# Expert weights by rank: W2 loaded in order of first use, W1 by id for 40 batches, b2's rows spread by GpSimd

## The chip, the cores and the metric

One core of one Trainium2 chip. The metric is device time in microseconds (us) of the kernel, median of its runs. The engines: TensorE (PE; PEld is its weight load), VectorE (DVE), ScalarE (ACT), GpSimd (POOL), SyncE (SP, which here only issues DMAs).

## What is computed

`x` is 128 batches of 128 x 512 float32; each batch has a language id, and each of `L = 10` languages its own small layer.

```python
w1 = W1[language_ids]                       # 512 x 128
w2 = W2[language_ids]                       # 128 x 512
h = relu(einsum('bsh,bha->bsa', x, w1) + b1[language_ids][:, None, :])
adapted = einsum('bsa,bah->bsh', h, w2) + b2[language_ids][:, None, :]
y = x + adapted
mean, var over the last axis of y
normed = (y - mean) * rsqrt(var + 1e-5)
out = x + normed * gamma[language_ids][:, None, :] + beta[language_ids][:, None, :]
```

## The kernel before, in words

A batch is one tile of 128 rows (partitions) by 512. Its steps, and the engine that does each:

- TensorE transposes x in four pieces (`transpose_x`, L235), ScalarE copies the result out of PSUM (`copy_xT`, L239).
- `down` (L258): four float32 matmuls with W1 of the batch's language. ScalarE applies relu and b1 (`relu`, L266).
- `up` (L275): the matmul with W2, read from `w2` at an offset that comes from the language id in a register.
- b2 is added in one of three ways: GpSimd adds it to x ahead of time (`add_b2`, L245, r = x + b2), or VectorE adds it to the result (`vector_b2`, L285), or TensorE adds it as a matmul that picks the row (`up`, L274). `b2_by_vector` and `b2_by_matmul` say which.
- VectorE: `residual` (L292, adds r or x and sums), `scale` (L358, minus the mean, times gamma), `finish` (L367, times the deviation, plus o). ScalarE: the squares (L315) and the root. GpSimd: `add_beta` (L252, o = x + beta).
- SyncE stores o in pairs of batches (L371) and loads x four batches at a time (`load_x`, L71).

gamma, beta (times -0.5 for gamma) and b2 have to stand on all 128 partitions (`gamma_b`, `beta_b`, `b2_b`, each 10 x 512 wide). At the start their 30 rows are split in three bfloat16 parts, and for each row a matmul with a picking column (`spread`, L206) spreads it over the partitions; VectorE (L211) or ScalarE (L209) copies it out of PSUM. The order is written out by hand ahead of the loop, beta's rows first, then gamma's, then b2's.

The loop `for i in range(3, B + U)` runs one batch per turn, software-pipelined: x of batch i, `down` of i-1, `up` of i-2, residual of b = i-3, `finish` one or two batches later; `add_b2(b + 2)` and `add_beta(b)` stand at the start of a turn. `keep` chains the instructions of each engine in program order, so that the scheduler changes nothing in it, the DMAs on SyncE's queue included. Buffers that set how far engines can run apart: 4 groups of x, 4 tiles r, 5 pairs o, 5 PSUM tiles of the result.

W1 reaches `down` in two ways. For batches 0 to 8 SyncE loads the matrix of the batch's own language from memory (`load_first`, L154, the id in a register). From batch 9 on ScalarE copies it (`stage_w1`, L226, 128x512) out of all ten, which lie in SBUF: `w1e` up to batch 20 (rows in the order "(p k)"), `w1` after. All of W2 is loaded at the start in two DMAs (L158).

A last stage (`tail`) finishes batches 124 to 127, partly on GpSimd (`by_pool`, L415, L417).

Of the kernel before, what the change touches and what calls it, by code (L numbers as in the profile page):

```python
# [16 lines left out]
P = 128  # L17
G = 4
EPS = 1e-5
FIRST = 9  # L20
EARLY = 21
LATE = 12
U = 2
# [3 lines left out]
def cond_resid_kernel(ctx: ExitStack, tc: tile.TileContext, x, itok, W1, b1, W2, b2, gamma, beta, out):  # L27
# [49 lines left out]

    ids = const.tile([1, B], I32, name="ids")
# [3 lines left out]
    w1e = const.tile([P, L, KC, A], FP, name="w1e")  # L82
    w2 = const.tile([P, L * H], FP, name="w2")
    x_0 = xp.tile([P, G, H], FP, tag="x", name="x_0")
    xs[0] = x_0

# [3 lines left out]

    keep(nc.sync.dma_start(out=ids, in_=itok.rearrange("(o b) -> o b", o=1)))
    keep(nc.scalar.dma_start(out=rows[0:L, :], in_=beta))
    keep(nc.sync.dma_start(out=rows[L : 2 * L, :], in_=gamma))
    keep(nc.scalar.dma_start(out=rows[2 * L : 3 * L, :], in_=b2))
    load_part(0, 2)
    keep(nc.scalar.dma_start(out=b1r, in_=b1))

    warm = const.tile([P, 1], FP, name="warm")
    keep(nc.vector.memset(warm, 1.0))
    keep(nc.scalar.activation(warm, warm, AF.Abs_reciprocal_sqrt))  # L100
    def load_w1(k):
        keep(
            nc.sync.dma_start(out=w1[:, :, k, :], in_=W1[:, k * P : (k + 1) * P, :].rearrange("l p a -> p l a"))
        )

    ident = const.tile([P, P], FP, name="ident")
    make_identity(nc, ident)
    eps = const.tile([P, 1], FP, name="eps")
    nc.gpsimd.memset(eps, EPS)
    ones = const.tile([P, P], BF, name="ones")  # L110
    nc.gpsimd.memset(ones, 1.0)

# [13 lines left out]

    wrap = const.tile([1, B], I32, name="wrap")
    keep(nc.vector.tensor_scalar(wrap, ids, 0, L, ALU.is_lt, ALU.mult))
    lang = const.tile([1, B], I32, name="lang")
    keep(nc.vector.tensor_tensor(lang, ids, wrap, ALU.add))  # L130
    keep(nc.vector.tensor_scalar(lang, lang, 0, L - 1, ALU.max, ALU.min))

    def lid(b, engine):
        g = b // G
        if (g, engine) not in lids:
            loads, vals = nc.values_load_multi_w_load_instructions(  # L136
                lang[0:1, g * G : (g + 1) * G],
                engines=[engine],
                min_val=0,
                max_val=L - 1,  # L140
                skip_runtime_bounds_check_because="clamped on the chip to 0..L-1 above",
            )
            for ins in loads:
                keep(ins)
            lids[g, engine] = vals
        return lids[g, engine][b % G]

    def load_first(b):
# [4 lines left out]
    def load_w2(lo, hi):  # L156
        dst = w2[:, lo * H : hi * H].rearrange("p (l h) -> p l h", l=hi - lo)
        keep(nc.sync.dma_start(out=dst, in_=W2[lo:hi].rearrange("l a h -> a l h")))  # L158

    def load_early(lo, hi):  # L160
        dst = w1e[:, lo:hi].rearrange("p l k a -> p l (k a)")
        keep(nc.sync.dma_start(out=dst, in_=W1[lo:hi].rearrange("l (p k) a -> p l (k a)", k=KC)))
# [8 lines left out]
    xs[1] = xp.tile([P, G, H], FP, tag="x", name="x_1")  # L171
    for b in (G, G + 2):
        load_part(b, b + 2)
        load_first(b)
        load_first(b + 1)
    xs[2] = xp.tile([P, G, H], FP, tag="x", name="x_2")
    load_part(2 * G, 2 * G + 2)
    load_early(0, 5)
    load_first(2 * G)
    load_early(5, L)  # L180
    load_part(2 * G + 2, 3 * G)

    left = rp.tile([P, H], FP, tag="r", name="left")
    keep(nc.vector.tensor_copy(parts[0:R, :], rows[0:R, :]))
    keep(nc.vector.tensor_tensor(left[32 : 32 + R, :], rows[0:R, :], parts[0:R, :], ALU.subtract))
    keep(nc.vector.tensor_copy(parts[32 : 32 + R, :], left[32 : 32 + R, :]))
    keep(nc.vector.tensor_tensor(left[64 : 64 + R, :], left[32 : 32 + R, :], parts[32 : 32 + R, :], ALU.subtract))
    keep(nc.vector.tensor_copy(parts[64 : 64 + R, :], left[64 : 64 + R, :]))

# [6 lines left out]


    beta_b = const.tile([P, L * H], FP, name="beta_b")
    gamma_b = const.tile([P, L * H], FP, name="gamma_b")
    b2_b = const.tile([P, L * H], FP, name="b2_b")  # L200

    def spread(r, copier):
        t = (beta_b, gamma_b, b2_b)[r // L]
        row = p_y.tile([P, H], FP, tag="y", name=f"row_{r}")
        pick_r = pick[:, r : r + 1].to_broadcast([96, P])
        keep(nc.tensor.matmul(row, lhsT=pick_r, rhs=parts[:96, :], start=True, stop=True))  # L206
        dst = t[:, r % L * H : (r % L + 1) * H]
        if copier is nc.scalar:
            keep(nc.scalar.copy(dst, row))  # L209
        else:  # L210
            keep(nc.vector.tensor_copy(dst, row))  # L211

    xT, hT, rs, os, ys, ssqs, nmeans, rstds = {}, {}, {}, {}, {}, {}, {}, {}
    phs, pxs, sums = {}, {}, {}


    def b2_by_matmul(b):
        return b in (5, B - 1)

    def b2_by_vector(b):  # L220
        return b < 4 or 8 <= b < B - 8 and (b % 4 == 1 if b < 24 else b % 16 in (1, 6, 11) or b % 32 == 30)

    def stage_w1(b):
        w1s[b] = wp.tile([P, KC, A], FP, tag="w1s", name=f"w1s_{b}")
        src = (w1e if b < EARLY else w1).rearrange("p l k a -> p (l k a)")[:, bass.ds(lid(b, ET.Activation) * (KC * A), KC * A)]
        keep(nc.scalar.copy(w1s[b].rearrange("p k a -> p (k a)"), src))  # L226

    def transpose_x(b):
        pxs[b] = p_x.tile([P, KC, P], FP, tag="xT", name=f"pxT_{b}")
        for k in range(KC):  # L230
            if b < EARLY:
# [36 lines left out]
    def up(b):  # L268
        v = lid(b, ET.PE)
        ys[b] = p_y.tile([P, H], FP, tag="y", name=f"py_{b}")  # L270
        m = b2_by_matmul(b)
        if m:
            pick_b = pick[:, bass.ds(v + 2 * L, 1)].to_broadcast([96, P])
            keep(nc.tensor.matmul(ys[b], lhsT=pick_b, rhs=parts[:96, :], start=True, stop=False))  # L274
# [214 lines left out]

    spin(9, H)  # L490
    spin(1, H // 2)

    def spread_turn(lo, hi):
        for r in range(lo, hi):
            spread(r, nc.scalar if r % 7 in (1, 3, 5) else nc.vector)

    def x_turn(b):
        transpose_x(b)
        copy_xT(b)

    x_turn(0)
    transpose_b1()
    spread_turn(0, 4)
    x_turn(1)
    spread_turn(4, 11)
    down(0)
    relu(0)
    spread_turn(11, 15)
    down(1)
    relu(1)  # L510
    x_turn(2)
    spread_turn(15, 19)
    x_turn(3)
    down(2)
    relu(2)
    spread_turn(19, 24)
    down(3)
    relu(3)
    spread_turn(24, R)
    up(0)  # L520
    up(1)

    for i in range(3, B + U):
        b = i - U - 1
        if b > G and b % G == 2 and b // G + 3 < NG:
            load_x(b // G + 3)
        if i == 5:
            load_x(3)
        if i in (8, 10, 12, 14):
            load_w1((i - 8) // 2)  # L530
        if i == 4:
            up(2)
        if i == 5:
            up(3)
        if i > 3 and on(i):
            transpose_x(i)
        if b <= E:
            add_b2(b + 2)
            add_beta(b)
        if i > 4 and on(i - 1):  # L540
            down(i - 1)
        if i > 3 and on(i):
            copy_xT(i)
        if b == 2:
            scalar_means(0)
            deviation(0)
        if i > 4 and on(i - 1):
            relu(i - 1)
        if i + 1 >= LATE and on(i + 1):
            stage_w1(i + 1)  # L550
        if i > 5 and on(i - U):
            up(i - U)
# [37 lines left out]
        if 0 < g and b <= E and half == 1:  # L590
            scalar_means(g)
            deviation(g)
        if FIRST <= i + 1 < LATE:
            stage_w1(i + 1)

        for n, engine in ((i + 3, ET.Activation), (i - U + 3, ET.PE), (b + 1, ET.DVE), (b + 5, ET.Pool)):
            if on(n):
                lid(n, engine)


# [35 lines left out]
```

## Time and profile before

| | |
|---|---|
| median of 3 runs | 308.49 us (308.26 to 308.88) |
| profiled execution, span from first to last instruction | 306.5 us |
| busy, share of the span: PE, DVE, ACT, POOL | 96, 97, 92, 93% |
| granted TensorE clock, mean | 0.989 |
| `add_beta` L252, 128 times; `add_b2` L245, 97 times | 173.9 and 135.7 us in records that overlap |
| `stage_w1` L226 ScalarE copy, mean of one | 612 ns |
| DMA moved | 77.85 MB, mean 254 GB/s |

The profile is of one execution, and its span is the only time that it gives of it: what lies ahead of the first and behind the last instruction makes the rest of the 308.49 us of the runs. A line of a group gives the source line, the engine, what is written from what, and the times. A line of a wait reads "who waits <- who ended it: us in total, times, longest". In the table of stages "(x12)" is a count of instructions. Names carry no buffer numbers: `r`, `o`, `x` stand for all of their kind, `b_b` for `b2_b`.

### The profile page before, as it was taken

The page shows a single profiled execution, that of the slowest core. Times are in us where ns is not written, and L with a number is a line of the kernel's source. Part 1 is how long each engine was busy: PE and PEld are TensorE (multiplying, and loading weights), DVE is VectorE, ACT ScalarE, POOL GpSimd, SP SyncE. Part 2 cuts the span into 40 slices and gives each one's busy share as a digit, 9 for nine tenths or more (in the row PEclk, how much of TensorE's full clock was granted, in tenths as well). Part 3 has the DMA queues.
Part 4 walks back from the last instruction along what each step waited for, and adds up shares of the span by engine and source line. Part 5 has one row for each costly group of instructions (what it writes and reads, how often), then busy time and mean ns, then how long its engine had stood idle before and what let it go on. Part 6 is the DMA issues. An engine that isn't in the chain of part 4 may idle for free. (4 is left out here: it accounts for less than half of the span.)

```text
span 306.5 us, 6981 instructions
## 1 busy us (share of the span) xinstructions
PE 294.6 (96%) x1835; PEld 220.0 (72%) x1835; DVE 295.9 (97%) x771; ACT 282.3 (92%) x777; POOL 283.9 (93%) x238
## 2 busy tenths in 40 slices
PE   8999999999999999999999999999999999999960
PEld 3748787777777777777777777777777777777730
DVE  6889999999999999999999999999999999999985
ACT  3858999999999999999999999999999999999981
POOL 1349899999999999999999999999999999999994
PEclk9999999999999999999999999999999999999995
DMA  6999999976678766766777666767776666773324
GB/s 231 379 390 388 373 371 354 387 231 240 221 255 276 250 202 241 226 257 219 259 276 243 213 209 238 265 224 260 275 238 206 226 231 242 246 266 137 135 109 171
DMA packets 43769, 77.85 MB, mean 254 GB/s; under 512 B 1961, under 2 KB 7348, under 8 KB 43730
## 3 DMA queue, kind: packets, MB, share of 16 engines
q1 hardware_dynamic: 43382, 76.84, 72.1%
q10 hardware_dynamic: 348, 0.57, 0.5%
q8 instruction: 15, 0.25, 0.3%
q14 instruction: 24, 0.20, 0.2%
HBM read 43.85 MB, written 33.55 MB: 253 GB/s over the span
## 5 line engine op out<-in xcount | busy, mean ns | idle before, releaser
L252 POOL TENSOR_TENSOR o<-x,beta_b 128x512 f32<-128x512 f32 x128 | 173.9, 1395 | 10.2 <-DVE beta_b L211 9.5
L245 POOL TENSOR_TENSOR r<-x,b_b 128x512 f32<-128x512 f32 x97 | 135.7, 1399 | 7.3 <-DVE b_b L211 6.2
L258 PE MATMUL ph<-xT,w1s 128*128 128x128 f32 x1024 | 135.4, 275 | 0.0
L275 PE MATMUL py<-w,hT 128*128 x256 | 131.2, 595 | 0.5 <-DVE b_b L211 0.5
L258 PEld LDWEIGHTS ph<-xT,w1s 128*128 128x128 f32 x1024 | 124.9, 192 | 1.0 <-ACT hT L266 0.5
L235 PEld LDWEIGHTS pxT<-ident,x 128*128 128x128 f32 x512 | 66.6, 151 | 65.3 <-issue 49.2
L358 DVE SCALAR_TENSOR_TENSOR py<-py,nmean,gamma_b 128x512 f32<-128x512 f32 x126 | 95.0, 754 | 0.9 <-ACT sq L399 0.8
L367 DVE SCALAR_TENSOR_TENSOR o<-py,rstd,o 128x512 f32<-128x512 f32 x122 | 91.2, 748 | 0.0
L315 ACT ACTIVATE sq<-py,sum 128x512 f32<-128x512 f32 x124 | 85.9, 693 | 2.8 <-DVE py L292 2.5
L235 PE MATMUL pxT<-ident,x 128*128 128x128 f32 x512 | 78.2, 276 | 0.0
L239 ACT COPY xT<-pxT 128x512 f32<-128x512 f32 x128 | 74.7, 584 | 3.5 <-PE pxT L235 3.5
L292 DVE SCALAR_TENSOR_TENSOR py<-py,r 128x512 f32<-128x512 f32 x97 | 67.0, 691 | 0.2
L226 ACT COPY w1s<-w 128x512 f32 x107 | 65.5, 612 | 0.0
L266 ACT ACTIVATE hT<-ph,b1T 128x128 f32<-128x128 f32 x128 | 46.9, 366 | 7.9 <-PE ph L258 2.6
L275 PEld LDWEIGHTS py<-w,hT 128*128 128x128 f32 x256 | 39.1, 192 | 2.9 <-issue 1.0
L315 ACT ACTIVATION_READ_ACCUMULATOR sq<-py,sum 128x1 f32 x124 | 25.0, 202 | 0.0
L292 DVE SCALAR_TENSOR_TENSOR py<-py,x 128x512 f32<-128x512 f32 x31 | 21.7, 699 | 0.4
L285 DVE TENSOR_TENSOR py<-py,b_b 128x512 f32<-128x512 f32 x29 | 20.2, 695 | 0.7 <-PE py L275 0.6
L325 ACT ACTIVATE root<-ssq,eps 128x2 f32<-128x2 f32 x62 | 16.4, 265 | 0.0
L292 DVE DVE_READ_ACCUMULATOR py<-py,r 128x1 f32 x97 | 13.7, 141 | 0.0
L306 ACT ACTIVATE nmean<-sum 128x2 f32<-128x2 f32 x62 | 12.3, 198 | 0.0
L329 DVE SCALAR_TENSOR_TENSOR part<-ssq,root 128x2 f32<-128x2 f32 x62 | 9.3, 151 | 0.2 <-ACT root L325 0.2
(55 smaller groups left out, 90.4 us busy)
## 6 DMA issues: line engine op xcount, KB each, us to landing
out_dram<-o SPq DMA_DIRECT2D x61, 512.0 KB, 3.4
x<-in_x_dram SPq DMA_DIRECT2D x29, 1024.0 KB, 6.2
x<-in_x_dram SPq DMA_DIRECT2D x6, 512.0 KB, 8.8
w1e<-in_L_cond_W_dram SPq DMA_DIRECT2D x2, 1280.0 KB, 12.3
w<-in_L_cond_W_dram SPq DMA_DIRECT2D x4, 640.0 KB, 8.1
w1s<-in_L_cond_W_dram SPq DMA_DIRECT2D x9, 256.0 KB, 8.4
w<-in_L_cond_W_dram SPq DMA_DIRECT2D x1, 1792.0 KB, 10.3
w<-in_L_cond_W_dram SPq DMA_DIRECT2D x1, 768.0 KB, 5.4
```

Of the source, the lines that this page charges most:

```text
L226: keep(nc.scalar.copy(w1s[b].rearrange("p k a -> p (k a)"), src))
L235: keep(nc.tensor.transpose(pxs[b][:, k, :], cols, ident))
L239: keep(nc.scalar.copy(xT[b], pxs.pop(b)))
L245: keep(nc.gpsimd.tensor_tensor(rs[b], xb(b), b2_b[:, bass.ds(v * H, H)], ALU.add))
L252: keep(nc.gpsimd.tensor_tensor(os[g][:, j, :], xb(b), beta_b[:, bass.ds(v * H, H)], ALU.add))
L258: nc.tensor.matmul(phs[b], lhsT=w1s[b][:, k, :], rhs=xT[b][:, k, :], start=(k == 0), stop=(k == KC - 1))
L266: keep(nc.scalar.activation(hT[b], phs.pop(b), AF.Relu, bias=b1T[:, bass.ds(lid(b, ET.Activation), 1)]))
L275: keep(nc.tensor.matmul(ys[b], lhsT=hT[b], rhs=w2[:, bass.ds(v * H, H)], start=not m, stop=True))
L292: nc.vector.scalar_tensor_tensor(ys[b], ys[b], 1.0, r, ALU.mult, ALU.add, accum_out=col(sums, b))
L315: nc.scalar.activation(sq, ys[b], AF.Square, bias=col(sums, b), scale=-float(H), accum_out=col(ssqs, b))
L358: nc.vector.scalar_tensor_tensor(ys[b], ys[b], col(nmeans, b), gamma_b[:, bass.ds(v * H, H)], ALU.add, ALU.mult)
L367: nc.vector.scalar_tensor_tensor(o, ys.pop(b), rstds[g][:, j : j + 1], o, ALU.mult, ALU.add)
```

## The change

- W2: instead of two large DMAs, ten DMAs of one language each, in the order in which the languages first appear. The order is worked out on the chip: for each language the first batch that has it (`seen`, `first`, VectorE), its rank among them (a matmul, `above` with `accum_out`), and from the ranks a row `slots` that holds for each place the language, and for each batch its place. SyncE reads the first, TensorE the second, in `up`. The ids are therefore on ten partitions, one for each language, and GpSimd makes the constants with `iota`.
- W1: loaded by id for batches 0 to 39 into a ring of 7 tiles; `w1e` is gone, `stage_w1` starts at batch 40, and `w1` is loaded in turns 16, 21, 26 and 31 rather than 8, 10, 12 and 14.
- b2: one DMA brings all ten rows to partition 0 of `b2_b`, and two `partition_broadcast` on GpSimd, each of 2560 words, spread them. They stand ahead of GpSimd's first add. The spread by matmul stays for 20 rows (beta, gamma), alternately copied by VectorE and ScalarE; the last 9 of them stand in the turns 3 to 5 of the loop.
- b2 of batches 0 to 3 by matmul rather than by VectorE; that of batch 5 by GpSimd rather than by matmul.
- The three casts for the bfloat16 parts become two copies on ScalarE and a subtraction that writes bfloat16. 6 idle matmuls at the start rather than 10.

```diff
-FIRST = 9
-EARLY = 21
-LATE = 12
+BY_ID = 40
+RING = 7
...
-    wp = ctx.enter_context(tc.tile_pool(name="wp", bufs=5))
+    wp = ctx.enter_context(tc.tile_pool(name="wp", bufs=RING))
...
+    keep(nc.scalar.dma_start(out=b2_b[0:1, :], in_=b2.rearrange("(o l) h -> o (l h)", o=1)))
...
+    nc.gpsimd.iota(weight, [[-16, B + 1]], base=16 * B, channel_multiplier=-1)
+    nc.gpsimd.iota(lang[:, B : B + 1], [[0, 1]], base=0, channel_multiplier=1)
+    nc.gpsimd.iota(count[:, 0:L], [[1, L]], base=0, channel_multiplier=0, allow_small_or_imprecise_dtypes=True)
+    nc.gpsimd.iota(count[:, L : L + 1], [[0, 1]], base=0, channel_multiplier=1, allow_small_or_imprecise_dtypes=True)
...
+    keep(nc.vector.scalar_tensor_tensor(seen, lang, own, weight, ALU.is_equal, ALU.mult))
+    keep(nc.vector.tensor_reduce(first, seen, mybir.AxisListType.X, ALU.max))
+    def rank_languages():
+        order = p_s.tile([P, H], FP, tag="s", name="order")
+        keep(nc.tensor.matmul(order[:L, 0:L], lhsT=first.to_broadcast([L, L]), rhs=ident[:L, :L], start=True, stop=True))
+        keep(nc.vector.tensor_tensor(rows[32 : 32 + R, :], rows[0:R, :], upper(rows, 0), ALU.subtract))
+        keep(nc.vector.tensor_scalar(above, order[:L, 0:L], first, None, ALU.is_gt, ALU.add, accum_out=rank))
+        keep(nc.vector.tensor_scalar(own_of, lang[:, 0:B], own, None, ALU.is_equal))
+        keep(nc.vector.tensor_scalar(place, count[:, 0:L], rank, None, ALU.is_equal))
+        keep(nc.vector.tensor_tensor(parts[64 : 64 + R, :], rows[32 : 32 + R, :], upper(rows, 32), ALU.subtract))
+        keep(nc.scalar.copy(parts[0:R, :], upper(rows, 0)))
+        keep(nc.scalar.copy(parts[32 : 32 + R, :], upper(rows, 32)))
+        return order
+    def place_languages(order):
+        keep(nc.tensor.matmul(order[:1, L : 2 * L], lhsT=own, rhs=place, start=True, stop=True))
+        keep(nc.tensor.matmul(order[:1, 2 * L : 2 * L + B], lhsT=rank, rhs=own_of, start=True, stop=True))
+        keep(nc.vector.tensor_copy(slots, order[:1, L : 2 * L + B]))
...
-    load_w2(0, 3)
-    load_first(0)
-    load_first(1)
-    load_part(2, G)
-    load_first(2)
-    load_first(3)
-    load_w2(3, L)
...
+    def load_slot(j):
+        if j == 0:
+            v = lid(0, ET.SP)
+        else:
+            if not perm:
+                perm.extend(values(slots[0:1, 1:L], ET.SP, L - 1))
+            v = perm[j - 1]
+        src = W2[bass.ds(v, 1)].rearrange("o a h -> a (o h)")
+        keep(nc.sync.dma_start(out=w2[:, j * H : (j + 1) * H], in_=src))
+    load_by_id(0)
+    load_slot(0)
+    load_by_id(1)
+    load_by_id(2)
...
+    def spread_b2(lo, hi):
+        cols = slice(lo * H, hi * H)
+        keep(nc.gpsimd.partition_broadcast(b2_b[:, cols], b2_b[0:1, cols]))
...
     def b2_by_matmul(b):
-        return b in (5, B - 1)
+        return b < 4 or b == B - 1
     def b2_by_vector(b):
-        return b < 4 or 8 <= b < B - 8 and (b % 4 == 1 if b < 24 else b % 16 in (1, 6, 11) or b % 32 == 30)
+        return 8 <= b < B - 8 and (b % 4 == 1 if b < 24 else b % 16 in (1, 6, 11) or b % 32 == 30)
...
     def up(b):
-        v = lid(b, ET.PE)
+        v = slot(b)
...
+    def ahead(n):
+        if n == 3:
+            load_slot(1)
+            load_part(4, 6)
+        elif n == 5:
+            load_part(6, 8)
...
+        load_by_id(n)
+        if 3 < n < L + 2:
+            load_slot(n - 2)
+    spread_b2(0, L // 2)
+    spread_b2(L // 2, L)
     x_turn(0)
     transpose_b1()
+    place_languages(order)
+    x_turn(1)
     spread_turn(0, 4)
...
-        if i in (8, 10, 12, 14):
-            load_w1((i - 8) // 2)
+        if i in (16, 21, 26, 31):
+            load_w1((i - 16) // 5)
...
+        if i + RING - 2 < BY_ID:
+            ahead(i + RING - 2)
+        if i < 6:
+            spread_turn(3 * i + 2, 3 * i + 5)
...
-        if i + 1 >= LATE and on(i + 1):
+        if BY_ID <= i + 1 and on(i + 1):
             stage_w1(i + 1)
```

More of the change, by code (lines that the diff above doesn't have):

```diff
@@ L75, in xb @@
         return xs[b // G][:, b % G, :]
-    ids = const.tile([1, B], I32, name="ids")
     rows = rp.tile([P, H], FP, tag="r", name="rows")
@@ L124, in cond_resid_kernel @@
     lids, w1s = {}, {}
[L127 to L131, printed above, removed]
+    wrap = st.tile([L, B], I32, tag="wrap", name="wrap", bufs=1)
+    keep(nc.vector.tensor_scalar(wrap, lang[:, 0:B], 0, L, ALU.is_lt, ALU.mult))
+    keep(nc.vector.tensor_tensor(lang[:, 0:B], lang[:, 0:B], wrap, ALU.add))
@@ new lines, in cond_resid_kernel @@
+    keep(nc.vector.tensor_scalar(lang[:, 0:B], lang[:, 0:B], 0, L - 1, ALU.max, ALU.min))
+    seen = st.tile([L, B + 1], FP, tag="seen", name="seen", bufs=1)
+    first = st.tile([L, 1], FP, tag="first", name="first", bufs=1)
+    rank = st.tile([L, 1], FP, tag="rank", name="rank", bufs=1)
+    above = st.tile([L, L], FP, tag="above", name="above", bufs=1)
+    place = st.tile([L, L], FP, tag="place", name="place", bufs=1)
+    own_of = st.tile([L, B], FP, tag="own", name="own_of", bufs=1)
+    slots = const.tile([1, L + B], I32, name="slots")
@@ L487, in spin @@
             )
[L490 to L495, printed above, removed]
+    spin(6, H)
+    order = rank_languages()
     def x_turn(b):
```

143 lines of the change are left out of this document (68 added, 75 removed).

## The prediction

> **What bounds the kernel now.** I read the table of stages first, then who waited for whom on GpSimd, its order of time at the start and near the end, the chain of waits, and the landings.
>
> The table of stages (length, then busy us and instructions of PE, PEld, DVE, ACT, POOL, clock, DMA share, GB/s):
>
> ```profile
> 0.00:10.00 10.00, 8.76 (x35) 4.39 (x36) 7.25 (x19) 4.85 (x9) 0.87 (x8) 1.00 0.74 270
> 10.00:20.00 10.00, 9.54 (x60) 6.57 (x59) 7.77 (x13) 7.04 (x15) 2.83 (x3) 1.00 1.02 381
> 20.00:30.00 10.00, 10.00 (x58) 7.26 (x57) 9.63 (x23) 7.41 (x21) 10.00 (x9) 1.00 1.05 388
> ...
> 110.00:290.00 180.00, 180.00 (x1151) 136.66 (x1150) 179.76 (x472) 176.33 (x493) 180.00 (x147) 1.00 0.68 232
> ```
>
> From 20 us on GpSimd (180.00 of 180.00) and VectorE (179.76) are both full; a free place exists only in the first 20 us. So the question is when each of the two gets its steady work, and how much of it there is. GpSimd's waits say that it never stops after that:
>
> ```profile
> POOL o L252 <- DVE beta_b L211: 9.5, 1, 9.5
> POOL r L245 <- DVE b_b L211: 6.2, 1, 6.2
> POOL r L245 <- DMA x<-in_x_dram: 1.1, 1, 1.1
> POOL o L252 <- DMA out_dram<-o: 0.5, 1, 0.5
> ```
>
> 9.5 and 6.2 us are waits for rows spread over the partitions; then 1.6 us in the remaining 287. In order of time:
>
> ```profile
> 0.93 0.20 POOL L111 MEMSET ones<- 128x128 bf16 x1
> 1.16 0.29 POOL masks.py:199 TENSOR_SCALAR_AFFINE_SELECT ident<-ident 128x128 f32<-128x128 f32 x1
> 10.98 2.50 POOL L252 TENSOR_TENSOR o<-x,beta_b 128x512 f32<-128x512 f32 x2 [9.53 <-DVE beta_b L211]
> 19.67 1.27 POOL L245 TENSOR_TENSOR r<-x,b_b 128x512 f32<-128x512 f32 x1 [6.19 <-DVE b_b L211]
> 20.89 2.51 POOL L252 TENSOR_TENSOR o<-x,beta_b 128x512 f32<-128x512 f32 x2
> ...
> 291.43 5.13 POOL L252 TENSOR_TENSOR o<-x,beta_b 128x512 f32<-128x512 f32 x4
> 296.34 1.45 POOL L415 TENSOR_TENSOR n<-n,gamma_b 128x512 f32<-128x512 f32 x1
> ```
>
> There are 225 adds (128 of beta, 97 of b2), 2 of them before 19.67. The other 223 fill 19.67 to 296.34, 276.67 us; less 1.6 us of waits that is 1.2335 us each, start to start (the 1.395 us of the page's groups overlap by what is left). The chain of waits ends on the same engine:
>
> ```profile
> 291.65 4.91 POOL o L252 x4
> 296.56 1.22 POOL n L415
> 297.79 0.04 issue
> 297.83 0.05 POOLq L415
> 297.87 1.25 POOL o L417
> ```
>
> So, with T the start of GpSimd's unbroken run of N adds, the span is T + 1.2335 N + waits + (306.5 - 296.34 = 10.16). Before: 19.67 + 275.1 + 1.6 + 10.16 = 306.5.
>
> **The change, part by part.** *GpSimd, adds.* Batch 5's b2 moves from TensorE to GpSimd, 0 to 3 move from VectorE to TensorE: 98 + 128 = 226 adds. All now stand behind the two broadcasts in GpSimd's order, so N = 226, 278.8 us. Span = T + 278.8 + 10.2 = T + 288.9, taking no waits on buffers (the engine will be behind, not ahead). Break-even with 306.5 is T = 17.6.
>
> *GpSimd, what stands ahead of T.* The affine select ends at 1.45. An iota of 10x129 and three tiny ones are not in the trace: by MEMSET 128x1 (0.10) and the select (0.29) they are 0.4 to 1.0 us, I take 0.7. GpSimd is at the broadcasts at 2.2.
>
> Two broadcasts of 2560 words: unknown. Below, MEMSET only writes: (0.204 - 0.098)/127 = 0.83 ns a word, 2.1 us. Above, the select reads one tile and writes one: (0.29 - 0.10)/128 = 1.5 ns, 3.9 us. An add (2.4 ns a word, 6.2 us) reads two and is farther off. I take 3.0 each, 6.0 together (4.2 to 7.8).
>
> Two changes of library: the built program has an instruction that reloads GpSimd's library by index ahead of the first broadcast (to library 1) and another behind the second, ahead of the first add (back to 0). The kernel before has one such instruction, to library 0, seen in the answer on the line of the select:
>
> ```profile
> masks.py:199 POOLq MODIFY_POOL_CONFIG  x2: 11/11/11, 1.1 to 1.1; - x2
> ```
>
> It cost nothing: the select starts 0.03 us behind the memset. But 0 was there already, so this is only the lower bound. A library that is not there has to be fetched, and fetches of that moment are in the list of landings (KB, then median us):
>
> ```profile
> out_dram<-o SPq DMA_DIRECT2D x61, 512.0 KB, 3.4
> w1e<-in_L_cond_W_dram SPq DMA_DIRECT2D x2, 1280.0 KB, 12.3
> w1s<-in_L_cond_W_dram SPq DMA_DIRECT2D x9, 256.0 KB, 8.4
> ```
>
> In the first 30 us the DMA engines are full (1.02 to 1.05); the smallest weight loads then take 8.4 us, stores in the calmer part 3.4, the longest loads 12.3. I take 8.4 for each change, nearest in moment and size. The Trainium skill (GPSIMD Engine Reference, Instruction dispatch) says that the first call to a freshly loaded kernel pays a load of about 6 us that shows as no instruction. By that figure (an estimate for both changes) T would be 2.2 + 6 + 6.0 + 6 = 20.2 and the time 311.1; no run so far shows it.
>
> T = 2.2 + 8.4 + 6.0 + 8.4 = 25.0, span 25.0 + 288.9 = 313.9. The median of the runs before, 308.49, lies 2.0 above the profiled span, so 315.9 us, 2.4% slower. The 15.7 us of waits for rows go, but T moves from 17.6 (what the old start is worth) to 25.0.
>
> *VectorE* loses 7 spread copies of 0.68 (17 to 10), the three casts (1.25), four adds of b2 (2.8), and gains six small operations (seen, reduce, above, own_of, place, slots; 0.2 each like wrap): 7.6 us less. That hides behind GpSimd: the first finish (batch 0) waits for the first add of beta, and the residual of batch 4 for r_4, both behind T. If GpSimd were early, this cover is gone and VectorE's own time counts: from its first residual (20.87) to the end it needed 285.6; less 2.8, plus 3 copies that now come later (2.0), 284.8. With the first residual at about 13 that ends at 298, still under the forecast by 16.
>
> *ScalarE* loses 28 copies of W1 for batches 12 to 39 (0.61 each, 17.1 us) and 3 row copies, gains two casts. Nothing comes of it: at 176.33 of 180 it is full too, but it is not what ends last.
>
> *TensorE*: ten row matmuls and four spins less, three for the ranking and net three of b2 more, and from 0 to 9 a load of a register each (0.33 on its queue) with nothing waiting behind it that GpSimd doesn't hold longer. Zero.
>
> *SyncE*: the load of slot 1 waits for the ranked slots, and with it x from batch 4 on and W1 from 3 on. The ranking ends at about 6 (five VectorE steps of 0.2 behind lang at 2.8, two of 0.68, three matmuls); 2 MB issued before it keep the engines busy to about 7 at 388 GB/s. Zero. If it came 2 us later, batch 4 would still be in by 13, before T.
>
> *Traffic*: 40 W1 loads (10.5 MB) replace 9 and w1e (5.0 MB). In batches 16 to 36 a batch needs x, W1 and a store (0.262 MB each) and its share of w1 (2.62 MB in 20), 0.917 MB in 2.2 us: 417 GB/s, over the 388 seen. That is 2.36 us a batch, 3.3 us over the stage (5.7 at the 369 of 30 to 55 us), held off by W1 six and x eight batches ahead. I take 0; the upper end goes into the range.
>
> **The rivals.** (1) The library changes cost little, as the 11 ns say: the broadcasts end at 8.2, beta's rows are the last (the old wait for them ended at 10.98), T = 11, span 299.9, 301.9 us, faster. For it: the only row of this kind. Against: that row changes nothing. It decides below (17.6 - 2.2 - 6.0)/2 = 4.7 us a change. (2) Only the way to library 1 is paid, 0 staying resident: T = 2.2 + 8.4 + 6.0 = 16.6, span 305.5, 307.5 us; a little faster, and same with small errors. (3) The traffic is the bound besides: the forecast plus 3.3 to 5.7, 319 to 322. Against it: the DMA was at 1.05 to 1.07 from 20 to 55 us before, and cost GpSimd only 1.1 us.
>
> **How the numbers follow.** Forecast 0.80, rival 1 0.05, rival 2 0.07, rival 3 0.08. The range: low, one change at 3.4 and broadcasts at 4.2: T = 18.2, 309.1; high, one change at 12.3 and broadcasts at 7.8: T = 30.7, 321.6, which takes in rival 3. So 309 to 322; outside are rivals 1 and 2 and a change far over 12 us. A measurement of this kernel can tell about 0.2%. Faster by more: rival 1 and most of rival 2, 0.09; within: 0.03; slower: 0.88.
>
> **What would show it.** On GpSimd: empty stretches of over 5 us ahead of the first broadcast and between the second and the first add of beta; the adds unbroken from about 25 us, 1.23 us apart; VectorE waiting for o or r from about 20 us on, and idle some microseconds in all; no wait for b2's rows. Wrong, if the first add of beta starts before 17.6, if the adds come farther apart than 1.25, or if W1 (by id) is what TensorE waits for between 40 and 90 us.

## The result and the profile after

The kernel after takes 316.82 us (median of 4 runs, 316.49 to 318.26), the kernel before, run beside it, 308.48 (308.26 to 308.88): a ratio of 1.028, 95% interval 1.026 to 1.030. The forecast was 315.9. The profiled execution took 316.75 us, its span is 314.8.

GpSimd in the kernel after, in order of time (start, busy us, operation, in brackets the idle time ahead and who is named as its releaser):

```profile
2.14 0.09 POOL L126 MEMSET eps<- 128x1 f32 x1
10.56 5.48 POOL L263 PARTITION_BROADCAST b_b<-b_b  x2 [8.34 <-DVE beta_b L253]
26.71 2.50 POOL L304 TENSOR_TENSOR o<-x,beta_b 128x512 f32<-128x512 f32 x2 [10.67 <-DMA w1s<-in_L_cond_W_dram]
...
305.38 1.40 POOL L467 TENSOR_TENSOR n<-n,gamma_b 128x512 f32<-128x512 f32 x1
```

The two waits in brackets are all that GpSimd has over 0.3 us. Both releasers are wrong: the first add needs neither a W1 matrix nor anything else that is late. Both stretches are the library changes. (The first broadcast also needs b2's row from memory, whose landing is not in the trace; a part of the 8.34 may be that.)

Front to 2.23, 8.34 empty, 5.48 for two broadcasts, 10.67 empty: T = 26.71. The 226 adds then run to 305.38, 278.67 us or 1.233 each, without one wait, and 9.42 us follow. That is the span: 26.71 + 278.67 + 9.42 = 314.8. The instruction that changes the library shows almost nothing of it, in the view of the first add's line (min/median/max ns, first and last start):

```profile
L304 POOLq MODIFY_POOL_CONFIG  x2: 127/127/127, 15.9 to 16.0; - x2
L304 POOLq EVENT_SEMAPHORE  x1: 9180/9180/9180, 6.6 to 6.6; - x1
```

127 ns at 16 us, and the first add 10.7 us later; beta's ten rows had been ready since 15.8 (end of the sequencer's wait, 6.6 + 9.18). The chain of waits of the kernel after ends as before, on GpSimd:

```profile
300.64 4.91 POOL o L304 x4
305.56 1.22 POOL n L467
306.87 1.25 POOL o L469
```

So far this is the forecast. But a second engine is late by nearly as much. The table of stages of the kernel after (length, busy us and instructions of PE, PEld, DVE, ACT, POOL, clock, DMA share, GB/s):

```profile
0.00:10.00 10.00, 6.67 (x24) 3.19 (x25) 4.90 (x19) 3.89 (x6) 1.39 (x12) 1.00 0.65 219
10.00:20.00 10.00, 9.85 (x52) 6.96 (x51) 5.10 (x9) 5.90 (x13) 5.48 (x2) 1.00 0.88 316
20.00:30.00 10.00, 8.97 (x52) 6.08 (x52) 5.74 (x15) 6.95 (x18) 3.29 (x3) 1.00 1.04 396
...
55.00:110.00 55.00, 53.60 (x332) 40.76 (x331) 52.72 (x136) 42.25 (x118) 55.00 (x46) 1.00 1.02 368
110.00:290.00 180.00, 180.00 (x1150) 135.81 (x1149) 179.65 (x469) 176.11 (x493) 180.00 (x147) 1.00 0.68 237
```

From 110 us on TensorE is at 180.00 of 180, like GpSimd, and so it was before. By the starts of its transposes its median turn from batch 44 on is 2.191 us in every kernel of this case, whether GpSimd is ahead of it or behind; that this pace is its own is argued from that. From 0 to 10 and 20 to 30 us it now does 24 and 52 matmuls (35 and 58 before), and from 55 to 110 us 332 (353), with the DMA engines at 1.02 (0.73). ScalarE's relu of the last batch shows what comes of it, in the order of time of the kernel before and of the kernel after:

```profile
294.80 0.36 ACT L266 ACTIVATE hT<-ph,b1T 128x128 f32<-128x128 f32 x1
```

```profile
302.21 0.36 ACT L318 ACTIVATE hT<-ph,b1T 128x128 f32<-128x128 f32 x1
```

7.4 us later. By the relus in the trace 2.9 of that is there at batch 4 (24.65 to 27.58), 1.3 comes from batch 4 to 16, 2.8 from 16 to 36, and 0.4 after; from batch 40 to 127 every kernel of this case takes 190.7 to 191.3 us. What TensorE loses early it never regains.

Most of what it loses from batch 8 to 40 stands on its queue. For every four batches TensorE loads four values from a row into registers, right ahead of its next transposes: the ids from `lang` before, the places from `slots` now. These loads in the kernel before and in the kernel after, from 36 us to 108 (min/median/max ns, first and last start), and the transposes behind the longest of them, which starts at 58.3 and ends at 60.7:

```profile
L136 PEldq TENSOR_LOAD <-lang x9: 331/333/782, 36.3 to 107.6; - x9
```

```profile
L183 PEldq TENSOR_LOAD <-slots x8: 1371/1749/2368, 40.0 to 105.3; - x8
...
60.89 0.72 PE L287 MATMUL pxT<-ident,x 128*128 128x128 f32 x4 [0.40 <-ACT sq L367]
```

In the kernel after, seven of the eight transposes behind these loads start 0.21 us behind the end of the load (in the kernel before 0.84 to 1.64), and their seven turns are together 3.4 us longer than the 2.22 of the others. From the transposes of batch 8 to those of batch 40 TensorE takes 75.1 us, 70.6 before: three quarters of this loss stand behind these loads. That the transposes wait for them is read from the times; no run moved the loads, and why they take so long is open. From 110 us on they take 1.0 us.

The runs together give a reading that I did not have: the span is the later of two ends, TensorE's (start of the last batch's relu + 11.4) and GpSimd's (start of the last add of beta + 10.3). The 11.4 is taken from the kernel e2 below and the 10.3 from the kernel after and e8 (10.65, 10.1); the others follow within 0.5 us. It is a fit to these runs, not a law, and it cannot tell which of two ends holds where they lie closer than that. The ratio is to the kernel before, run beside each (308.4 to 308.7).

| kernel (profiled execution) | TensorE's end | GpSimd's end | span | median us | ratio, 95% |
|---|---|---|---|---|---|
| before | 306.2 | 305.4 | 306.5 | 308.48 | |
| after | 313.6 | 314.5 | 314.8 | 316.82 | 1.028 (1.026 to 1.030) |
| e1 broadcasts into the kernel before | 310.7 | 311.8 | 311.9 | 313.51 | 1.017 (1.014 to 1.020) |
| e2 after, b2 by DMA | 313.6 | 312.1 | 313.6 | 315.29 | 1.022 (1.020 to 1.024) |
| e4 after, four adds to VectorE | 315.9 | 314.4 | 315.9 | 316.58 | 1.025 (1.022 to 1.028) |
| e5 e2, W1 by id to 20 | 310.9 | 311.4 | 311.7 | 313.62 | 1.019 (1.015 to 1.023) |
| e6 e2, rows first | 307.9 | 309.4 | 309.5 | 314.51 | 1.022 (1.017 to 1.027) |
| e7 e5 and e6 | 311.8 | 312.4 | 312.6 | 313.85 | 1.018 (1.012 to 1.025) |
| e8 e7 with the broadcasts | 310.8 | 314.7 | 314.5 | 315.95 | 1.025 (1.020 to 1.030) |
| e9 e6, 14 loads of W1 less | 309.1 | 307.7 | 309.0 | 311.11 | 1.008 (1.006 to 1.010) |
| e10 after, with e4, e9 and rows first | 314.0 | 312.6 | 314.5 | 316.96 | 1.028 (1.023 to 1.032) |
| e11 before, b2 of 0 to 7 by TensorE | 306.6 | 309.6 | 309.7 | 311.67 | 1.010 (1.008 to 1.012) |
| e12 e6, 27 loads of W1 less | 310.9 | 309.5 | 311.2 | 311.62 | 1.008 (1.005 to 1.011) |

The medians are of other executions too, and some kernels scatter: e6 from 311.3 to 317.3 (its profiled one is the fastest), e9 from 310.7 to 316.5, e2 only from 314.6 to 315.5.

### The profile page after: what moved, and what is told of

It is laid out like the page before. It is cut to its first block, busy times and chain, and to the rows that moved or that the text cites. A ratio compares the mean times of both kernels' runs of the same rounds, so it can differ in the third digit from the quotient of the medians.

```text
span 314.8 us, 7127 instructions
## 1 busy us (share of the span) xinstructions
PE 296.9 (94%) x1830; PEld 220.8 (70%) x1830; DVE 290.9 (92%) x764; ACT 270.4 (86%) x745; POOL 291.1 (92%) x245
## 5 line engine op out<-in xcount | busy, mean ns | idle before, releaser
L304 POOL TENSOR_TENSOR o<-x,beta_b 128x512 f32<-128x512 f32 x128 | 163.4, 1290 | 10.7 <-DMA w1s<-in_L_cond_W_dram 10.7
L327 PE MATMUL py<-w,hT 128*128 (+1 forms) x256 | 131.4, 595 | 0.0
L297 POOL TENSOR_TENSOR r<-x,b_b 128x512 f32<-128x512 f32 x98 | 126.3, 1289 | 0.0
L287 PEld LDWEIGHTS pxT<-ident,x 128*128 128x128 f32 x512 | 68.3, 161 | 70.4 <-issue 43.8
L291 ACT COPY xT<-pxT 128x512 f32<-128x512 f32 x128 | 74.9, 585 | 10.6 <-PE pxT L287 10.6
L287 PE MATMUL pxT<-ident,x 128*128 128x128 f32 x512 | 79.9, 279 | 2.5 <-DMA x<-in_x_dram 1.0
L344 DVE SCALAR_TENSOR_TENSOR py<-py,r 128x512 f32<-128x512 f32 x98 | 67.7, 691 | 2.7 <-POOL r L297 1.4
L278 ACT COPY w1s<-w 128x512 f32 x88 | 54.0, 613 | 0.0
L337 DVE TENSOR_TENSOR py<-py,b_b 128x512 f32<-128x512 f32 x25 | 17.3, 691 | 1.1 <-PE py L327 0.8
L263 POOL PARTITION_BROADCAST b_b<-b_b x2 | 5.5, 2800 | 8.3 <-DVE beta_b L253 8.3
```

The source lines that it names most:

```text
L291: keep(nc.scalar.copy(xT[b], pxs.pop(b)))
L297: keep(nc.gpsimd.tensor_tensor(rs[b], xb(b), b2_b[:, bass.ds(v * H, H)], ALU.add))
L304: keep(nc.gpsimd.tensor_tensor(os[g][:, j, :], xb(b), beta_b[:, bass.ds(v * H, H)], ALU.add))
L327: keep(nc.tensor.matmul(ys[b], lhsT=hT[b], rhs=w2[:, bass.ds(v * H, H)], start=not m, stop=True))
L344: nc.vector.scalar_tensor_tensor(ys[b], ys[b], 1.0, r, ALU.mult, ALU.add, accum_out=col(sums, b))
```

## The experiments

**e1: the broadcasts alone, in the kernel before.** The ten spreads of b2 by matmul stay (their copies are simply done once more).

```diff
+    keep(nc.scalar.dma_start(out=b2_b[0:1, :], in_=b2.rearrange("(o l) h -> o (l h)", o=1)))
+    for cols in (slice(0, L * H // 2), slice(L * H // 2, L * H)):
+        keep(nc.gpsimd.partition_broadcast(b2_b[:, cols], b2_b[0:1, cols]))
     x_turn(0)
```

> The kernel before, and nothing of the change but the load of b2's rows to partition 0 and the two broadcasts of 2560 words ahead of GpSimd's first add (the spread by matmul stays and writes the same values over them). Theory 1, the two changes of GpSimd's library and the broadcasts set when its unbroken run of adds starts: from the changed kernel's trace 8.3 us ahead of the first broadcast, 5.5 for both, 10.7 behind them, so the first add starts at 1.45 + 24.5 = 26.0, then 225 adds of 1.2335 and 10.2 to the end: span 313.7, time 315.7, ratio 1.023. Theory 2, the loss comes from the rest of the change (W1 by id and its traffic, the ranking that SyncE waits for, the slower start of TensorE): none of that is here, ratio 1.00 to 1.003.

Measured: 313.51 us, +5.1. GpSimd in order of time in e1:

```profile
10.62 5.48 POOL L503 PARTITION_BROADCAST b_b<-b_b  x2 [8.92 <-DVE beta_b L212]
24.97 2.49 POOL L253 TENSOR_TENSOR o<-x,beta_b 128x512 f32<-128x512 f32 x2 [8.88 <-DVE b_b L212]
```

The same two empty stretches, 8.92 and 8.88, in a kernel with nothing else of the change. T = 24.97, and T + 225 x 1.234 + 9.2 is its span of 311.9. The kernel is slower by 1.4 to 2.0%, less than the kernel after: T is 1.7 earlier and there is one add less.

GpSimd's own sum gives the span. What the run does not show is the broadcasts by themselves, because TensorE is late in it too, and not through GpSimd's adds. Its seven row matmuls and the `down` of batch 0, in the kernel before and in e1:

```profile
7.92 1.78 PE L206 MATMUL row<-parts,pick 96*128 96x512 bf16 x7
9.54 1.05 PE L258 MATMUL ph<-xT,w1s 128*128 128x128 f32 x8
```

```profile
7.36 1.10 PE L236 MATMUL pxT<-ident,x 128*128 128x128 f32 x4 [1.74 <-DMA x<-in_x_dram]
11.13 3.09 PE L207 MATMUL row<-parts,pick 96*128 96x512 bf16 x7
14.06 1.06 PE L259 MATMUL ph<-xT,w1s 128*128 128x128 f32 x8
```

Behind a wait of 1.74 us for x its first ten row matmuls take about 630 ns each (380 in the kernel before), at a granted clock of 1.00 in the stages of both, and the `down` of batch 0 is 4.5 us late, before the broadcasts have ended (16.1). That is the whole lateness of TensorE's end in the table (310.7 against 306.2), which GpSimd's end exceeds by 1.1. The first row matmuls of the kernel after are as slow (634 ns). Why x comes later in e1 was not tried.

**e2: the kernel after without the broadcasts.** b2's rows come by one DMA with a partition step of zero, behind the third W1 on SyncE's queue; it writes 2.6 MB, which is traffic of its own in the first 20 us.

```diff
-    keep(nc.scalar.dma_start(out=b2_b[0:1, :], in_=b2.rearrange("(o l) h -> o (l h)", o=1)))
+    keep(nc.sync.dma_start(out=b2_b, in_=b2.rearrange("(o l) h -> o (l h)", o=1).to_broadcast([P, L * H])))
-    spread_b2(0, L // 2)
-    spread_b2(L // 2, L)
```

> The changed kernel with the two broadcasts left out and b2 spread over the partitions by one DMA of 2.6 MB on SyncE's queue, behind the third W1 load, where the changed kernel's DMA had room (222 and 241 GB/s in the first two slices). No change of library is left. Theory 1: the first add waits for the last row of beta alone (copied at 15.9 in the changed kernel), then 226 adds of 1.2335 and 9.4 to 10.2 to the end: span 304 to 304.8; VectorE, with its first residual at 19.1 and 284.8 of its own from there, ends at 303.9 too, so some waits of one for the other: time 306.5 to 308.5, ratio 0.993 to 1.000 against before. Theory 2, the rest of the change costs the time: it stays at 312 or more, ratio over 1.01.

Measured: 315.29 us, 1.5 less than the kernel after. The theory that GpSimd alone is late falls. GpSimd's waits in e2:

```profile
POOL o L304 <- ACT beta_b L251: 11.3, 1, 11.3
POOL r L297 <- DMA x<-in_x_dram: 4.0, 1, 4.0
POOL r L297 <- DVE py L344: 3.8, 2, 2.6
POOL o L304 <- DMA out_dram<-o: 2.8, 3, 1.2
```

The first add starts at 13.2 rather than 26.7, and then GpSimd waits 10.6 us in all for x, for a free r and for stores: others are late now. The relu of the last batch starts at 302.16 us, hardly before that of the kernel after (302.21).

**e3: the library change by itself.** Only GpSimd works: broadcast (2560 words) and add (c = a + a, 128x512) in turn, three times with the DMA engines idle, three times while all of x is loaded. Nothing else of the computation is done.

```diff
+    def stretch(n):
+        for _ in range(n):
+            keep(nc.gpsimd.partition_broadcast(row, row[0:1, :]))
+            keep(nc.gpsimd.tensor_tensor(c, a, a, ALU.add))
+    stretch(3)
+    ...
+    stretch(3)
```

> Only the disputed cost, the layer is left out: three times a broadcast of 2560 words and an add of 128x512 on GpSimd with no traffic, then the same three times while SyncE loads x without a pause. Theory 1, a change of library is a fetch that costs what the traffic makes of it: idle time ahead of each broadcast and each add, some 6 us without traffic (the Trainium skill, GPSIMD Engine Reference, Instruction dispatch, says about 6) and 8 to 11 with it. Theory 1b: a fixed cost, 8.3 to library 1 and 10.7 back to library 0, with and without traffic. Theory 2, the idle time in the changed kernel was a wait for beta's rows and for data, not the library: under 1 us here.

GpSimd in order of time in e3; its DMA engines were at 0.00 up to 35 us and at 1.05 (387 to 388 GB/s) from 60 to 110 us:

```profile
24.02 2.80 POOL L63 PARTITION_BROADCAST row<-row  x1 [5.89 <-issue]
34.30 1.03 POOL L64 TENSOR_TENSOR c<-a 128x512 f32<-128x512 f32 x1 [7.48 <-issue]
...
81.06 2.80 POOL L63 PARTITION_BROADCAST row<-row  x1 [6.85 <-issue]
92.29 1.03 POOL L64 TENSOR_TENSOR c<-a 128x512 f32<-128x512 f32 x1 [8.43 <-issue]
```

Without traffic the way to the broadcast costs 5.9 to 6.0 us and the way back to the add 6.9 to 7.5, each time anew; under traffic 6.6 to 7.9 and 7.5 to 10.5. Nothing here waits for data. The cost belongs to the change of operation, not to something fixed at the start, and traffic adds to it. The Trainium skill (GPSIMD Engine Reference, Instruction dispatch) gives about 6 us for the first call to a freshly loaded kernel; the quiet way to the broadcast agrees (5.9 to 6.0), the way back and both ways under load are longer, and the 311.1 us that its figure gave in the prediction is 5.7 too low.

**e4: four adds moved from GpSimd to VectorE**, b2 of batches 11, 15, 19 and 23, in the kernel after.

```diff
-        return 8 <= b < B - 8 and (b % 4 == 1 if b < 24 else b % 16 in (1, 6, 11) or b % 32 == 30)
+        return 8 <= b < B - 8 and (b % 4 in (1, 3) if b < 24 else b % 16 in (1, 6, 11) or b % 32 == 30)
```

> The changed kernel with the b2 of four batches (11, 15, 19, 23) added by VectorE rather than by GpSimd. Theory 1, GpSimd's run of adds is the bound from its first add to the tail: 222 adds rather than 226, 4 x 1.233 = 4.9 us less, VectorE takes four more of 0.69 in time it has to spare (290.9 busy of 314.8): span 309.9, time 311.9, ratio 1.011. Theory 2, the end is set by traffic or by the slow start: within 1 us of 316.8, ratio 1.024 to 1.03.

Measured: 316.58 us, no gain that can be seen. Less work for GpSimd did not make an earlier end. In its profiled execution TensorE was later still (last relu at 304.5; granted clock 0.89 and 0.77 in the first two stages of 10 us, 1.00 in the kernel after), and GpSimd, with four adds less, waited 3.4 us for stores and 1.0 for a free r.

**e5: in e2, W1 by id only up to batch 20**, `w1` loaded in turns 8 to 14 as before the change.

```diff
-BY_ID = 40
+BY_ID = 21
-        if i in (16, 21, 26, 31):
-            load_w1((i - 16) // 5)
+        if i in (8, 10, 12, 14):
+            load_w1((i - 8) // 2)
```

> The kernel with b2 by DMA (no change of library), and W1 by id only for batches 0 to 20, ScalarE copies from 21, the whole of W1 loaded in turns 8 to 14: about the traffic of before. Theory A, two limits of about the same size stood in the changed kernel, GpSimd's late adds and W1's traffic with a slow first 30 us; with the first gone, traffic sets batches 4 to 40 (their residuals come 2.31 us apart, 2.21 before). Then the residual of batch 20 still comes at 67.7, but batch 40's at 112 rather than 114.4: time 313, ratio 1.014 to 1.018. Theory B, traffic is no limit, all is lost in the first 30 us: within 0.7 us of 315.3.

Measured: 313.62 us, near the expected 313, 1.7 under e2; the intervals of the two ratios overlap. The residual of batch 40 comes at 111.9 (112 expected). From batch 16 to 36 TensorE took 45.3 us rather than 47.1 (44.1 before).

**e6: in e2, all twenty rows spread ahead of the loop**, none in turns 3 to 5.

```diff
-    spread_turn(8, 11)
+    spread_turn(8, 2 * L)
-        if i < 6:
-            spread_turn(3 * i + 2, 3 * i + 5)
```

> The kernel with b2 by DMA, and the nine rows of gamma that the turns 3 to 5 spread moved ahead of the first matmul with W2, as in the kernel before. Theory A: the turns 3 to 5 take 3.5 us each because the rows and the results share five PSUM tiles and their copies stand ahead of the copy of x; without them the residual of batch 4 comes at 28 to 29.5 rather than 31.3, but the traffic up to batch 40 gives a part of it back: time 312.5 to 315, ratio 1.013 to 1.021. Theory C, what is late at batch 4 is the load of W2's slots and W1 (0.77 MB a batch, behind the 2.6 MB of b2): the residual of batch 4 stays at 31, time within 0.7 us of 315.3.

Measured: 314.51 us, 0.8 under e2 and too scattered for a verdict on the time. On the front it is plain. One turn of TensorE from transpose to transpose, in order of time in e2 (without its `down` and `up`):

```profile
24.33 0.63 PE L287 MATMUL pxT<-ident,x 128*128 128x128 f32 x4
...
25.69 0.60 PE L248 MATMUL row<-parts,pick 96*128 96x512 bf16 x2
26.75 0.38 PE L248 MATMUL row<-parts,pick 96*128 96x512 bf16 x1 [0.46 <-ACT gamma_b L251]
...
28.41 0.63 PE L287 MATMUL pxT<-ident,x 128*128 128x128 f32 x4
```

and in e6:

```profile
12.47 3.19 PE L248 MATMUL row<-parts,pick 96*128 96x512 bf16 x12
...
17.37 0.64 PE L287 MATMUL pxT<-ident,x 128*128 128x128 f32 x4
...
19.81 0.63 PE L287 MATMUL pxT<-ident,x 128*128 128x128 f32 x4
```

With three rows in it, a turn is 4.1 us from transpose to transpose, 0.46 of it a wait for ScalarE's copy out of PSUM; without them 2.44. Twelve rows in one go take 3.19 us. The relu of batch 4 starts at 23.8 in e6 and at 28.4 in e2. Not all of the 4.6 is the rows' own work: in e2 TensorE also waits 2.3 us for W2 ahead of the loop, and its granted clock is 0.90 from 10 to 20 and 0.93 from 20 to 30 us, against 1.00 in e6.

**e7: e5 and e6 together.**

> b2 by DMA, W1 by id only up to batch 20, gamma's rows ahead of the first matmul with W2: all three suspected limits eased. Theory A, they are what the time went to: the residual of batch 4 at 28 to 29.5, then 2.21 us a batch: 309 to 311.5, ratio 1.002 to 1.010. If it stays over 313, something else sets the pace.

Measured: 313.85 us, outside the expected range: the gains do not add. The front is right (batch 4 at 23.9), but then TensorE loses 2.5 us more from batch 4 to 16 than in e5 (29.0 against 26.5) and 2.1 more from 16 to 36 (47.4 against 45.3), with the same four loads of `w1` in turns 8 to 14. In three of these turns, batches 12, 16 and 20, its transposes start 0.21 us behind a register load; they are 3.6 us too long in all.

**e8: e7 with the broadcasts of the kernel after.**

> The changed kernel with its broadcasts and changes of library, and the two other limits eased (W1 by id up to batch 20, gamma's rows ahead). Theory A, GpSimd's late run of adds alone is enough to hold the end: first add at 26 to 27, 226 adds of 1.233 and 9.4, span 313.8 to 315.1, time 315.5 to 317, ratio 1.023 to 1.028, no gain. Theory B, the rest of the change alone cost the time: like the kernel with the same and b2 by DMA, 311.5 or less.

Measured: 315.95 us, as expected. GpSimd in order of time in e8:

```profile
11.71 5.48 POOL L263 PARTITION_BROADCAST b_b<-b_b  x2 [9.49 <-DVE beta_b L253]
27.03 2.50 POOL L304 TENSOR_TENSOR o<-x,beta_b 128x512 f32<-128x512 f32 x2 [9.84 <-DMA w<-in_L_cond_W_dram]
```

TensorE is 2.8 us earlier than in the kernel after (last relu at 299.4), and the span is 314.5 against 314.8: here GpSimd holds the end alone, 3.9 us behind TensorE's by the table. Beside e2, where by the table TensorE's end holds it at 313.6, 1.5 behind GpSimd's, this is the main finding: with either one as late as this the kernel is about 7 us slower than before (e8 7.3, e2 6.9), and taking away one of them gives back 1 to 2.

**e9: in e6, 14 loads of W1 less**: odd batches from 13 on use the matrix of the batch before.

```diff
+        if b > 12 and b % 2:
+            w1s[b] = w1s[b - 1]
+            return
```

> As the kernel with b2 by DMA and gamma's rows first (W1 by id for 40 batches), but from batch 13 on every odd batch uses the W1 of the batch ahead of it and loads none: 14 of the 40 loads (3.7 MB) and their use are left out, so this is only of use for its time. Theory A, the traffic is the second limit: DMA share under 1 somewhere between 50 and 100 us, residuals of batches 12 to 40 no more than 2.22 us apart, GpSimd's waits for stores and x under 3 us: time 308.5 to 311, and the executions agree within 1 us (that kernel's spread over 6). Theory D, the traffic only went along and the front still costs it: within 1 us of 314.5.

Measured: 311.11 us, a little over the expected top; 3.4 under e6, and the ratios' intervals lie apart. GpSimd's waits in e6 and in e9:

```profile
POOL o L304 <- DMA out_dram<-o: 4.6, 7, 1.4
POOL r L297 <- DMA x<-in_x_dram: 2.9, 1, 2.9
```

```profile
POOL r L300 <- DVE py L347: 2.5, 3, 1.3
POOL r L300 <- DMA x<-in_x_dram: 1.4, 1, 1.4
POOL o L307 <- DMA out_dram<-o: 0.5, 1, 0.5
```

Only the loads differ. With all 40 GpSimd waits 4.6 us for stores to free o tiles; with 26 it is 0.5, as in the kernel before, but 2.5 us of waits for a free r are new. So the traffic of W1 by id has a price by the medians. Where it is paid the two profiled executions do not show: their spans are 309.5 and 309.0, and TensorE takes 81.5 and 81.3 us from batch 4 to 40 in them.

**e10: the kernel after with the rows first, 14 loads of W1 less, and e4's four adds moved.**

> The changed kernel with its broadcasts, gamma's rows first, W1 for odd batches from 13 on left out as before, and the b2 of four batches moved from GpSimd to VectorE. Theory A, with the second limit gone the first one counts by itself: first add at 27.0, 222 adds of 1.2331, 9.4 to the end: span 310.1, time 312, ratio 1.010 to 1.014; the same four adds that gained nothing in the changed kernel now give their 4.9 us against the 315.95 of the kernel with both eased. Theory D: 315 or more.

Measured: 316.96 us; missed by 5. GpSimd's end is 312.6 in the table, 2.5 later than expected: it waited 2.9 us for a free r and for stores. TensorE's is later still (314.0): it took 48.0 us from batch 16 to 36. Its longest wait there, 1.61 us, ends at 71.29, and the register load ahead of it, of 2.53 us, 0.2 us sooner. Four such turns (batches 16, 20, 24 and 28) are together 3.3 us longer than 2.22 each. That the loads are the cause is argued from these times; no run took it apart.

**e11: a version meant to beat the kernel before**: b2 of batches 0 to 7 by TensorE, so that GpSimd has three adds less early (4, 6 and 7); three others, of batches 30, 62 and 94, go from VectorE to GpSimd.

```diff
-        return b in (5, B - 1)
+        return b < 8 or b == B - 1
-        return b < 4 or 8 <= b < B - 8 and (b % 4 == 1 if b < 24 else b % 16 in (1, 6, 11) or b % 32 == 30)
+        return 8 <= b < B - 8 and (b % 4 == 1 if b < 24 else b % 16 in (1, 6, 11))
```

> A version from what was found: the kernel before, with b2 of batches 0 to 7 by matmul (it was 5 alone; 0 to 3 were VectorE's, 4, 6, 7 GpSimd's) and b2 of 30, 62 and 94 by GpSimd rather than VectorE. No library, no new traffic. VectorE: 7 adds of 0.69 less, 4.8 us. GpSimd: 225 adds as before, but six of beta come ahead of the first that needs b2's rows, which then waits 1.3 us rather than 6.2: 219 from 19.67 on rather than 223, 4.9 us less. TensorE gets 7 row matmuls of 0.21 to 0.38 in the first turns, where it has room, and then has to run at 2.16 us a batch, as it can by its 2.15 of issue. Expected: span 301.7 to 303.5, time 303.7 to 305.5, ratio 0.985 to 0.990. If TensorE or ScalarE holds 2.20 us a batch, 306.5 to 308.

Measured: 311.67 us, slower by 0.8 to 1.2%. GpSimd's waits in e11:

```profile
POOL r L245 <- DMA x<-in_x_dram: 9.4, 2, 6.4
...
POOL o L252 <- DMA x<-in_x_dram: 2.3, 1, 2.3
```

GpSimd ran ahead of the loads and waited 11.7 us for x that had not landed: the adds that it gave up early became waits, and the three taken on later stayed. TensorE did not go faster either: its median turn is 2.191 us, as in every kernel here, not the 2.16 that was expected. No version of this study beats the kernel before.

**e12: in e6, batches 13 to 39 use batch 12's W1** (27 loads, 7.1 MB less).

```diff
+        if b > 12:
+            w1s[b] = w1s[b - 1]
+            return
```

> As the kernel with b2 by DMA and gamma's rows first, but batches 13 to 39 use the W1 of batch 12 and load none: 27 of the 40 loads (7.1 MB) and their use are left out. All three suspects are then gone: GpSimd's library, the rows in the first turns, the traffic of W1 by id. Theory A (TensorE runs at 2.197 us a batch in every kernel and keeps what it loses): relu of batch 4 at 24 to 25, of batch 40 79.2 to 80 later as in the kernel before (81.4 with half of these loads, 83.4 in the changed kernel), the end 11.7 behind the relu of batch 127 or GpSimd's own 13.8 to 15 + 278.7 + 9.4 with 1 to 3 of waits, whichever is later: span 306 to 307.5, time 308 to 309.5, ratio 0.998 to 1.003. If batch 40 still comes 81 or more behind batch 4, something other than W1's loads slows batches 4 to 40.

Measured: 311.62 us (309.5 to 313.4): only the fastest execution reached the expected range. In the profiled one TensorE took 30.9 us from batch 4 to 16 (27.5 in e6), and 44.5 from 16 to 36. Two turns, of 4.5 and 3.9 us, make most of this loss: ahead of batch 12 it waits 1.42 us behind a register load of 2.29 us, and its matmuls right after that are slow, with a granted clock of 0.83 from 40 to 50 us:

```profile
40.58 1.10 PE L290 MATMUL pxT<-ident,x 128*128 128x128 f32 x4 [1.42 <-issue]
41.47 1.92 PE L313 MATMUL ph<-xT,w1s 128*128 128x128 f32 x8
```

With the broadcasts, the rows in turns and 27 of the 40 loads all gone, 0.5 to 1.1% are still lost. The loads from `slots` are still there; whether they are all of the rest was not tried.

## Why the prediction was right, and where it was not

The sign and the mechanism on GpSimd hold, and so does the number, but the number by itself proves little: in e2, without any library change, the time is 315.29, nearer to the forecast of 315.9 than that of the kernel after. What shows the mechanism is the trace, with its two empty stretches and the adds behind them, e3 and e8. None of the three things came that would have made it wrong: the first add was late, the adds 1.233 us apart, and TensorE waited for W1 0.5 us in all from 40 to 90 us. The picture of the other engines does not hold.

- *Two library changes, 8.4 each*: 8.34 and 10.67. Shown by e3, and by the same two stretches in e1 and e8. That the DMA engines are full in the first 30 us is misread: the prediction's own table has 0.74 for the first 10. The second change is the term that was mis-sized, by 2.3.
- *Two broadcasts, 6.0*: 5.48 (2.80 recorded, 2.74 start to start), 1.07 ns a word, between the memset and the select as bounded.
- *226 adds at 1.2335 without a wait*: 226 at 1.233, no wait. *Tail 10.16*: 9.42. The errors in T (+1.7) and in the tail (-0.7) partly cancel, and the span came out 0.9 over the 313.9.
- *Rivals 1 and 2* (changes cost little, or only one does): excluded by the two empty stretches. Rival 1's T of 11 was too early in any case: beta's rows were ready at 15.8.
- *"With the cover gone VectorE ends at 298", and rival 1's 301.9*: wrong. In e2 GpSimd is early and the span is 313.6. The sum asked for VectorE's busy time from its first residual on, and not when TensorE would hand over the products. The table of stages shown in the prediction has 180.00 for TensorE as well as for GpSimd; only GpSimd and VectorE were read as full. By the table above, the two ends of the kernel before lie 0.8 us apart, TensorE's the later; its chain of waits ends on GpSimd, so which of them held it is not shown.
- *TensorE "zero"*: its matmuls are fewer, but their place costs. Moving nine rows out of turns 3 to 5 brings batch 4 forward by 4.6 us (e2 to e6), by 1.6 with the broadcasts there (after to e8). The register loads, priced at 0.33 each, are that for the single ones up to batch 9 (0.30 to 0.33); the loads of four from `slots`, from batch 10 on, take 1.0 to 2.4 us, and stand ahead of 3.4 us of lost time. And while W1 comes by id a turn takes 2.22 us rather than 2.19, up to batch 39 rather than 20: 0.6 us more. The loads of four are the term that was left out.
- *ScalarE "28 copies of W1"*: 31 (119 to 88), those of batches 9 to 11 too. Nothing hangs on it.
- *SyncE "zero, the ranking ends at about 6"*: the slots are cast at 8.2, SyncE reads the nine of them until 10.4 (one record of 1.87 us) and its queue stands still from 6.1 to 10.6, with the DMA engines at 0.65 in this stage (0.74 before), by SyncE's order of time in the kernel after. One reason is seen ahead of it: b1's transpose stands before the ranking's matmuls on TensorE and waits for its rows until 7.3. What this pause costs was not tried.
- *Traffic, taken as 0, 3.3 as its bound*: the sum of 2.36 us a batch was near: from batch 16 to 36 47.1 in e2 and 46.8 in the kernel after, 44.0 to 44.1 in e8 and before. The loss lies on TensorE and beside GpSimd's, not on top of it, so rival 3 was wrong as a time. It does not go with the number of W1's loads alone: e6 has all of them and lost only 0.8 there, e10 has two thirds of them and lost 3.9. By the times it goes mostly with the register loads: those of e6 take 1.0 us for the most part, with its DMA engines as full (1.05 to 1.08 from 20 to 90 us). What makes them long stays open.
- *VectorE waiting for o or r from about 20 us, "idle some microseconds in all"*: it waits for r only 1.4 us by the profile. The named waits for GpSimd are small because TensorE was late too.

## What to carry to other kernels

Price a GpSimd operation of another library by both changes, to it and back, at their length under the traffic of that moment: two broadcasts of 5.5 us together held GpSimd for 24.5 here, ahead of work in which it had no slack. When several engines run at full busy time, the wait that a change causes on one of them is only the first limit; compute the end of each full engine separately, from when it gets its steady work, and expect that undoing one cause gives back only the distance to the next. Time that TensorE lost in the first 40 turns stayed lost in every kernel here. Look for it on its queue as well as among its matmuls: a register load that took 0.33 us and cost nothing took up to 2.4 us when its source changed, and stood ahead of the work.

## What was not expected of the hardware

- The library change is invisible as an instruction (127 ns) and shows as idle time that the profile puts down to whatever landed last: a DMA of W1, a copy of VectorE.
- The way back to the add is the dearer one: 6.9 to 7.5 us quiet, against 5.9 to 6.0.
- GpSimd's add of 128x512 took 1.03 us with nothing beside it (e3, one input read twice) and 1.233 start to start in these kernels.
- Loading four values from `lang` into TensorE's registers took 0.33 us, four from `slots` 1.0 at the least and up to 2.5 (e10).
- Executions of one kernel lay up to 6 us apart (e6), those of e2, with its DMA engines as full (1.02 to 1.07 from 20 to 100 us), 0.9. The reason is open.
